# Second attention: feature forms of q and k by transposes of the token forms instead of a second projection

## The chip, the cores and the metric

One Trainium2 chip; the kernel runs on one of its cores. A core has a matrix engine (TensorE, "PE" in the profile), a vector engine (VectorE, "DVE"), an activation engine (ScalarE, "ACT"), a general engine (GpSimd, "POOL"), and a sync engine (SyncE, "SP") that issues most transfers. Each works through its own queue in order. The metric is the device time of one execution in microseconds. Before the change the median of three runs was 689.84 us (688.49 to 690.34).

## The reference, cut to what matters

Two layers. Each takes a layer norm of x, an attention s of it and a gated expert network g, and returns x + s * silu(g). x is 4 batches of 512 tokens with 128 features. The change lies in the attention of the second layer, which has 16 heads of 8 features and 16 channels:

```python
def proj(W, b):
    y = jnp.einsum('bse,ef->bsf', x, W) + b
    return y.reshape(B, S, H, D).transpose(0, 2, 1, 3)
Q = proj(Wq, bq)
K = proj(Wk, bk)
V = proj(Wv, bv)
cos_pm = jnp.cos(phase_modulators)

def wl_step(acc, wl):
    cpm, iw = wl
    m = cpm[None, :, None, None]
    scores = jnp.einsum('bhqd,bhkd->bhqk', Q * m, K * m) * SCALE
    scores = scores * jnp.cos(KERR * scores * scores)
    out = jnp.einsum('bhqk,bhkd->bhqd', jax.nn.softmax(scores, axis=-1), V)
    return (acc + out * iw, None)
```

The channels differ in a factor on the scores alone. The kernel computes a few functions of the scores (two exponentials, and powers up to the cube) once, and mixes them for each channel.

## The kernel before

The program is one stream of instructions for each engine, in an order that the code writes down: the helpers `mm1`, `act1`, `vec1`, `pool1` and `dma1` pin what they issue to the order of the program, so an instruction that waits holds up everything behind it on its engine. Most of them record one line each for all their calls (L356 for matmuls, L359 for activations, L379 for SP's transfers), so the profile is read by tile names.

It has three stages: the first layer up to about 303 us, the experts of the second layer (`ffn1`, 303 to 409 us), and the second attention (`attn1`, from 409 us).

**What a batch of the second attention needs.** `prepare1(b, ...)` gives the preparation of batch b as a table of steps, numbered by when they run. A step is a matmul part, an optional eviction and a rest.

- `tokens(w)`: the token form, tokens on the partitions. Four matmuls into the PSUM tile `ptq`, `ptk` or `ptv`; DVE adds the bias (L1407). Of k it makes the tile `tokk`, which holds every feature twice for the cubes; of q the tile `tokq`, which POOL squares (L1419); of v the values in `strip`.
- `project(w)`: the feature form, features on the partitions. One matmul of 512 columns from the same normed input into `pjq` or `pjk`; ACT adds the bias `b1` and evicts it to `qT` or `kT`. POOL then splits it into three bf16 parts (L1486, L1488: `part0` to `part2`, with the rest of the split in `left`), and SP writes the parts to DRAM (`kd`, `qd`). Of q, SP also writes tables of the feature form (`qe`, `qf`, in `table`).
- `cubes`, `forms`, `turned`: the products of the features of k (DVE, tile `feat`), sums of them over the tokens (PE, `pl`), and their transposes (PE, `pf`; DVE, `lin`).
- `sizes(w)`: bounds of the sums of squares (DVE).

The part tiles have one buffer each, so the first part of q waits until that of k has been written to DRAM. `spare` hands out the tiles `tokq` and `left` from two buffers.

**When the steps run.** Batch 0 is prepared in `ffn1`, one step for each expert pair from position 5 of `between` on (`prep`, `prepare`), as PE, ACT and DVE go through the experts; the first step of batch 1, `tokens("k")`, comes last. In `attn1`, iteration i of 64 does 16 iterations for each batch: four matmuls for scores (`s`), 32 for the sums over the keys (`acc`), the exponentials and squares (`e`) on ACT, some of the squares on DVE. In it, iteration t of batch b runs step t of batch b+1 and step t-16 of batch b+2, and `mixing`, which turns the sums of a finished head group into outputs:

- t = 8 `bank1` (`b`), 10 `sums1` (`den`; DVE takes the reciprocal `inv`), 11 `output1` of the batch before (`po`, `y`), 13 and 14 `quotients1` (`mix`; DVE multiplies to `pr`).

All the matmul parts of steps and mixing share the tag "mix" with two buffers. The matmul part of iteration i is issued in it, its rest in iteration i+1. The loads from DRAM (`first`, `second`, `third`, and `k`, `q`) stand in SP's queue at fixed iterations, between the writes of the preparation.

The table of steps (L1592):

```python
steps = {
    -7: [tokens("k")], -4: [], 0: [tokens("v"), project("k"), cubes(0)], 1: [project("q")],
    2: [forms(0), cubes(1)], 3: [tokens("q")], 4: [forms(1), cubes(2)],
    5: [sizes("k")], 6: [sizes("q")], 7: [turned(0), forms(2), cubes(3)],
    9: [forms(3)], 10: [turned(1)],
}
```

For b > 1, step -4 also holds the second half of the products of k (`quads`, L1429).

Of the kernel before, what the change touches and what calls it, by code (L numbers as in the profile page):

```python
# [12 lines left out]
F32 = mybir.dt.float32  # L13
# [4 lines left out]
ALU = mybir.AluOpType  # L18
# [3 lines left out]
P = 128  # L22
# [80 lines left out]
def bc(ap, axis, n):  # L103

    shape = list(ap.shape)
    return ap.unsqueeze(axis).to_broadcast(shape[:axis] + [n] + shape[axis:])


class Kernel:
# [124 lines left out]
    def load_second(self, pool, aside):  # L234

        nc, i = self.nc, self.i
        self.w1, self.b1, self.wt, self.bt = {}, {}, {}, {}
        for w in ("q", "k", "v"):
            own = aside.tile([P, D], F32, name=f"l1w{w}")
            nc.sync.dma_start(out=own, in_=i[f"L1_attn_W{w}"])  # L240

            flat = aside.tile([P, D], F32, name=f"l1b{w}f")
            nc.gpsimd.dma_start(out=flat, in_=i[f"L1_attn_b{w}"].partition_broadcast(P))
            self.wt[w] = pool.tile([P, D], F32, name=f"l1w{w}t")
            self.bt[w] = pool.tile([P, D], F32, name=f"l1b{w}t")
            for to, src in ((self.wt[w], own), (self.bt[w], flat)):
                nc.gpsimd.tensor_copy(
                    to.rearrange("p (m r d) -> p m r d", m=4, r=4),
                    src.rearrange("p (r m d) -> p m r d", m=4, r=4),
                )  # L250
            if w != "v":
                self.b1[w] = pool.tile([P, 1], F32, name=f"l1b{w}")
                own = i[f"L1_attn_b{w}"].rearrange("(r m d o) -> m r d o", m=4, r=4, o=1)
                for m in range(4):
                    nc.gpsimd.dma_start(out=self.b1[w][m * 32 : m * 32 + 32], in_=own[m])
        self.b1["o"] = pool.tile([P, D], F32, name="l1bo")
        nc.gpsimd.dma_start(out=self.b1["o"], in_=i["L1_attn_bo"].partition_broadcast(P))
        self.load_phases(aside)

        self.pm_hw = pool.tile([P, 2], F32, name="pm_hw")  # L260
        self.iw_hw = pool.tile([P, 1], F32, name="iw_hw")
        phases = i["L1_attn_phase_modulators"].rearrange("w (q m o) -> o q w m", o=2, q=4)

        self.wo_rep = pool.tile([P, 4, D], F32, name="wo_rep")
        nc.gpsimd.memset(self.wo_rep, 0.0)
        wo = i["L1_attn_Wo"].rearrange("(q u d) f -> q d u f", u=4, q=4)
        for q in range(4):
            for o in range(2):
                rows = slice(o * 64 + q * WL, o * 64 + (q + 1) * WL)
                nc.gpsimd.dma_start(out=self.pm_hw[rows], in_=phases[o, q])  # L270
                nc.gpsimd.dma_start(
                    out=self.iw_hw[rows], in_=i["L1_attn_interference_weights"].unsqueeze(1)
                )
            for j in range(3):
                at = q * 32 + j * 9
                nc.sync.dma_start(out=self.wo_rep[at : at + D1], in_=wo[q])
# [1097 lines left out]
    def prepare1(self, b, xnT, psum, tag):  # L1374
# [11 lines left out]
        def spare(what):  # L1386
            return pool.tile([P, S], F32, name=f"{what}{b}", tag="left", bufs=2)
# [8 lines left out]
        def tokens(w):  # L1396
            def pe():
                ps = psum.tile([P, 4, D], F32, name=f"pt{w}{b}", tag=tag[0], bufs=tag[1])
                for k in range(4):
                    self.mm1(  # L1400
                        ps[:, k, :], lhsT=toks[:, k, :], rhs=self.wt[w],
                        start=True, stop=True,
                    )
                return ps

            def biased(dst, ps):
                self.vec1(nc.vector.tensor_tensor(  # L1407
                    dst, ps.rearrange("p k (h d) -> p k h d", d=D1),
                    bc(self.bt[w].rearrange("p (h d) -> p h d", d=D1), 1, 4), ALU.add,
                ))  # L1410

            def rest(ps):
                if w == "v":
                    biased(own[:, :, :, 0:D1], ps)
                    return
                if w == "q":
                    t = spare("tokq").rearrange("p (n d) -> p n d", d=D1)
                    biased(t.rearrange("p (h k) d -> p k h d", k=4), ps)
                    self.pool1(nc.gpsimd.tensor_mul(t, t, t))  # L1419
                    now["squares" + w] = t  # L1420
                    return
                twice = pool.tile([P, 4 * H1, 2 * D1], F32, name=f"tok{w}{b}", tag="tok")
                t = twice[:, :, 0:D1]
                biased(t.rearrange("p (h k) d -> p k h d", k=4), ps)
                eng, pin = (nc.gpsimd, self.pool1) if b < 2 else (nc.vector, self.vec1)
                pin(eng.tensor_copy(twice[:, :, D1 : 2 * D1], t))

                def quads(at):
                    pin(eng.tensor_tensor(  # L1429
                        feat[:, :, at : at + 4], bc(t, 2, 4), moved(twice, SECOND[at], 2, 4),  # L1430
                        ALU.mult,
                    ))
                now["squares" + w], now["twice_k"] = feat[:, :, 0], twice
                now["quads"] = quads
                quads(0)
                if b < 2:
                    quads(4)
            return pe, rest
# [4 lines left out]
        def sizes(w):  # L1443
            def rest(_):
                size = pool.tile([P, H1, 4], F32, name=f"size{w}{b}", tag="size")
                self.vec1(nc.vector.tensor_reduce(
                    size.rearrange("p h k -> p (h k)"), now["squares" + w], AX.X, ALU.add
                ))
                self.vec1(nc.vector.tensor_reduce(
                    norms[:, int(w == "k"), b], size, AX.X, ALU.max  # L1450
                ))
            return (lambda: None), rest

        def project(w):
            def pe():
                ps = psum.tile([P, S], F32, name=f"pj{w}{b}", tag=tag[0], bufs=tag[1])
                self.mm1(ps, lhsT=self.wt[w], rhs=toks, start=True, stop=True)
                return ps

            def evict(ps):  # L1460
                t = pool.tile([P, S], F32, name=f"{w}T{b}", tag=f"{w}T")
                self.act1(t, ps, AF.Identity, bias=self.b1[w])
                return t

            def rest(t):
                if w == "q":


                    now["once"] = self.a1d.tile(
                        [4, D1, 4, S], F32, name=f"qe{b}", tag="qe"  # L1470
                    )
                    now["table"] = self.a1d.tile(
                        [4, TABLE, 2, 4, S], F32, name=f"qf{b}", tag="qf"
                    )
                    now["rows"] = t
                    if b == 0:
                        for m in range(4):
                            table(m)[1](None)

                dram = now["parts" + w] = self.a1d.tile(  # L1480
                    [P, 2, 4, S], BF16, name=f"{w}d{b}", tag=f"{w}d"
                )
                left = spare("left" + w)
                for k in range(3):
                    part = pool.tile([P, S], BF16, name=f"part{w}{b}_{k}", tag=f"part{k}")
                    self.pool1(nc.gpsimd.tensor_copy(part, t))  # L1486
                    if k < 2:
                        self.pool1(nc.gpsimd.tensor_sub(left, t, part))  # L1488
                        t = left
                    for x, at, end, step in STAND[w][k]:  # L1490
                        n = len(range(at, end, step))
                        self.dma1(dram[:, x, at:end:step], bc(part, 1, n))
            return pe, rest, evict

        def table(m):
# [70 lines left out]
        def turned(mm):  # L1566
# [23 lines left out]


        steps = {  # L1592
            -7: [tokens("k")], -4: [], 0: [tokens("v"), project("k"), cubes(0)], 1: [project("q")],
            2: [forms(0), cubes(1)], 3: [tokens("q")], 4: [forms(1), cubes(2)],
            5: [sizes("k")], 6: [sizes("q")], 7: [turned(0), forms(2), cubes(3)],
            9: [forms(3)], 10: [turned(1)],
        }
# [806 lines left out]
    def run(self):  # L2404
# [15 lines left out]
        with tc.tile_pool(name="wf1", bufs=1) as wf1, tc.tile_pool(name="f1", bufs=1) as f1:  # L2420
# [13 lines left out]
            with tc.tile_pool(name="ap", bufs=1, space=PSUM) as psum:  # L2434
# [13 lines left out]
                def begin():  # L2448
# [10 lines left out]
                    for at, each in steps.items():  # L2459
                        prep.extend(each if at == 0 else [each] if each else [])  # L2460
                    ahead = self.prepare1(1, first.xnT, psum, ("w", 4))
                    prep.extend([ahead[-7]])

                def prepare():
                    each = prep.pop(0)
# [26 lines left out]
                    18: [(f.up2, B - 1, NE // 2 - 1), (self.opening1, psum, "w", 4)],  # L2492
                    19.5: [(self.opened1, psum, "w", 4)],
                }
                for k in range(14):
                    between.setdefault(5 + k, []).append((prepare,))
                for k in range(4):
                    between.setdefault(13 + k, []).append((f.fetch, 1, 2 * k, 2))
# [75 lines left out]
```

## Time and profile before

| what | value |
| --- | --- |
| median of three runs | 689.84 us |
| the profiled execution | 691.6 us, of it span 689.9 us |
| chain that ended last | PE 74%, DVE 14%, ACT 8%, DMA 2% of the span |
| pjq and pjk (8 matmuls) | 16 records, 592 ns median |
| ptq, ptk, ptv | 32 records each, 275 ns median |
| kT, qT (ACT) | 4 each, 0.70 and 0.69 us |
| tokk, tokq (DVE, biased) | 4 each, 0.69 us |
| squares of q (POOL) | 4, 1.04 to 1.21 us |

A matmul of f32 leaves two records in the profile, a transpose of f32 one. Records of PE overlap, so what a group takes is read from its start to the start of the next one, not from the durations. "Idle before" in a line is the time that the engine waited ahead of the instruction, with what ended it. The span is that of the core's instructions; the execution's time has 1.7 us around it.

### The profile page before, as it was taken

The numbers are of one execution on the slowest core, as the hardware profiler recorded it, in microseconds if no ns is written. First come the engines' busy times: TensorE is split into PE (matmuls) and PEld (weight loads), VectorE is DVE, ScalarE is ACT, GpSimd is POOL, SyncE is SP. The second block draws the span as 40 slices with busy tenths as digits, with TensorE's granted clock in tenths as the row PEclk, the third lists the DMA queues.
The fourth block names the chain that finished last, engine by engine and source line by source line (L and its number), as shares of the span: only waits on it lengthen the run. The fifth ranks groups of instructions, "written<-read, shape, count | busy, mean of one in ns | idle before, by whom it ended". The sixth has DMA issues, their size and how long they took to land.

```text
span 689.9 us, 23790 instructions
## 1 busy us (share of the span) xinstructions
PE 656.5 (95%) x10123; PEld 411.0 (60%) x10123; DVE 501.9 (73%) x1084; ACT 487.2 (71%) x806; POOL 349.1 (51%) x383
## 2 busy tenths in 40 slices
PE   8999999999999898899999999999999999999995
PEld 4666667988978768777778863333335243422424
DVE  6866476686677958865378225979898999678884
ACT  4433478797787787643554369988997999899850
POOL 7590046767767575873753243312584753321170
PEclk9999999999999999999999999999999999999998
DMA  6850153233233131100034359777849694956300
GB/s 169 155 149 0 68 150 96 49 110 95 51 105 99 35 95 34 34 2 1 4 122 159 96 164 251 204 192 162 236 153 212 154 243 133 223 137 164 77 17 20
DMA packets 85489, 79.72 MB, mean 116 GB/s; under 512 B 42640, under 2 KB 74160, under 8 KB 82304
## 3 DMA queue, kind: packets, MB, share of 16 engines
q1 hardware_dynamic: 82544, 75.39, 41.5%
q0 software_dynamic: 2256, 2.47, 1.9%
q8 instruction: 82, 1.34, 0.8%
q10 hardware_dynamic: 576, 0.26, 0.2%
q14 instruction: 31, 0.25, 0.1%
HBM read 51.62 MB, written 26.21 MB: 113 GB/s over the span
## 4 chain that ended last, share of the span: by engine, by line
PE 74%; DVE 14%; ACT 8%; DMA 2%; issue 1%; POOL 0%; SPq 0%; DVEq 0%; ACTq 0%; POOLq 0%
PE acc L356 9%; PE eo L356 8%; PE pp L356 7%; ACT e L359 7%; PE po L356 6%; PE ph L356 5%; PE pv L356 4%; PE b L356 3%; PE s L356 3%; PE pl L356 3%; PE dot L356 2%; PE pg L356 2%; PE pu L356 2%; PE sc L356 2%; DVE elu L709 2%; PE mu L356 2%
## 5 line engine op out<-in xcount | busy, mean ns | idle before, releaser
L359 ACT ACTIVATE e<-s 128x1024 f32<-128x1024 f32 x124 | 122.2, 1059 | 14.5 <-PE s L356 14.1
L356 PE MATMUL acc<-e,strip 128*32 128x512 f32 x1000 | 123.7, 598 | 0.9 <-DVE e L1969 0.9
L359 ACT ACTIVATE e<-e 128x1024 f32<-128x1024 f32 x104 | 107.4, 1095 | 0.0
L763 POOL TENSOR_TENSOR t<-t,gate 128x512 f32<-128x512 f32 x32 | 52.3, 1634 | 52.8 <-DVE t L744 52.8
L356 PEld LDWEIGHTS acc<-e,strip 128*32 128x32 f32 x1000 | 28.2, 109 | 70.0 <-issue 59.0
L801 POOL TENSOR_TENSOR t<-t,gate 128x512 f32<-128x512 f32 x32 | 50.1, 1566 | 25.9 <-DVE sums L800 22.2
L359 ACT ACTIVATE pj<-pp 128x512 f32<-128x512 f32 x64 | 38.5, 602 | 19.3 <-PE pp L356 17.7
L709 DVE SCALAR_TENSOR_TENSOR elu<-elu,up 128x512 f32<-128x512 f32 x60 | 47.5, 791 | 0.2
L359 ACT ACTIVATE h<-ph 128x1024 f32<-128x1024 f32 x20 | 20.5, 1025 | 35.9 <-PE ph L356 32.1
L356 PE MATMUL s<-q,k 64*128 64x512 bf16 x256 | 41.1, 382 | 3.6 <-ACT e L359 3.3
L356 PEld LDWEIGHTS <-k 64*128 64x128 bf16 x256 | 8.7, 94 | 59.9 <-issue 58.1
L802 POOL TENSOR_TENSOR t<-t,t 128x512 f32<-128x512 f32 x32 | 42.2, 1320 | 2.5
L686 DVE TENSOR_TENSOR E<-sc,cap 128x512 f32<-128x512 f32 x32 | 22.0, 688 | 29.0 <-PE sc L356 29.0
L356 PE MATMUL eo<-w_out,h 128*128 128x128 f32 x320 | 39.7, 278 | 0.0
L356 PEld LDWEIGHTS eo<-w_out,h 128*128 128x128 f32 x320 | 37.7, 192 | 3.4 <-issue 2.4
L359 ACT ACTIVATE elu<-pj 128x512 f32<-128x512 f32 x60 | 38.5, 642 | 0.1
L359 ACT ACTIVATE up<-pj 128x512 f32<-128x512 f32 x60 | 38.4, 640 | 0.0
L1750 POOL TENSOR_TENSOR pr<-pr,pr 128x512 f32<-128x512 f32 x14 | 22.5, 1632 | 30.5 <-DVE pr L1745 30.4
L359 ACT ACTIVATE attT<-tn 128x128 f32<-128x128 f32 x100 | 19.6, 282 | 20.9 <-PE tn L722 19.9
L356 PE MATMUL pp<-xnT,l0Wk 128*64 128x128 f32 x512 | 31.4, 280 | 3.0 <-issue 2.2
L1657 DVE TENSOR_TENSOR second<-second,first 128x1024 f32<-128x1024 f32 x16 | 26.7, 1672 | 9.6 <-DMA second<-qf 9.6
L356 PE MATMUL po<-l0wo,attT 64*128 64x128 f32 x512 | 31.9, 281 | 0.3 <-DVE t L744 0.3
(353 smaller groups left out, 1589.4 us busy)
## 6 DMA issues: line engine op xcount, KB each, us to landing
vd<-vt SPq DMA_DIRECT2D x32, 256.0 KB
vone<-vd SPq DMA_DIRECT2D x64, 128.0 KB
first<-qe SPq DMA_DIRECT2D x8, 1024.0 KB
second<-qf SPq DMA_DIRECT2D x16, 512.0 KB
third<-qf SPq DMA_DIRECT2D x32, 256.0 KB
qf<-qT SPq DMA_DIRECT2D x64, 64.0 KB
k<-kd SPq DMA_DIRECT2D x16, 256.0 KB
q<-qd SPq DMA_DIRECT2D x16, 256.0 KB
```

Source lines behind the costliest of these rows:

```text
L356: return self.pin(self.nc.tensor.matmul(*args, **kw))
L359: return self.pin(self.nc.scalar.activation(*args, **kw))
L686: self.vec1(nc.vector.tensor_tensor(e, ps[:, :, 0:256].rearrange("p x (hp c) -> p x hp c", hp=4), bc(bc(self.cap, 1, 4), 1, 2), ALU.min,))
L709: self.vec1(nc.vector.scalar_tensor_tensor(t, t, 1.0, up, ALU.min, ALU.add))
L763: nc.gpsimd.tensor_mul(t, t, self.gate)
L801: nc.gpsimd.tensor_mul(t, t, gate2)
L802: nc.gpsimd.tensor_add(t, t, seg[n]["t1"])
L1657: self.vec1(self.nc.vector.tensor_mul(t, t, self.first1[mm][:, two]))
L1750: self.nc.gpsimd.tensor_add(self.prod1[b, m], self.prod1[b, m], t)
```

## The change

The bias of the feature form and its loads go: `b1` of q and k, eight small DMAs issued by POOL. `tokens` now keeps a token form with the features of each head group side by side, (k h d), as `tokens` + w: for q in place of the former order, for k by a second biased add from the same PSUM tile. `project` makes the feature form from it by four 128x128 transposes, and ACT evicts with Copy and no bias. The first squares of q on POOL move behind the split of q, since the transposes read the token form; `sizes("q")` reads them in the new order. The split of k subtracts in place. `tokens("q")` moves from step 3 to step -4: for batch 0 from behind `forms(0)` to behind `tokens("k")`, for batch 1 to the end of `ffn1`, for batches 2 and 3 to iteration 12 of the batch two before. In `ffn1`, `tokens("v")`, both `project`, `cubes(0)` and `forms(0)` of batch 0 each come one position later.

```diff
-            if w != "v":
-                self.b1[w] = pool.tile([P, 1], F32, name=f"l1b{w}")
-                own = i[f"L1_attn_b{w}"].rearrange("(r m d o) -> m r d o", m=4, r=4, o=1)
-                for m in range(4):
-                    nc.gpsimd.dma_start(out=self.b1[w][m * 32 : m * 32 + 32], in_=own[m])
...
                 if w == "q":
-                    t = spare("tokq").rearrange("p (n d) -> p n d", d=D1)
-                    biased(t.rearrange("p (h k) d -> p k h d", k=4), ps)
-                    self.pool1(nc.gpsimd.tensor_mul(t, t, t))
-                    now["squares" + w] = t
+                    t = now["tokens" + w] = spare("tokq").rearrange(
+                        "p (k h d) -> p k h d", k=4, d=D1
+                    )
+                    biased(t, ps)
                     return
...
                 biased(t.rearrange("p (h k) d -> p k h d", k=4), ps)
+                now["tokens" + w] = spare("tokk").rearrange("p (k h d) -> p k h d", k=4, d=D1)
+                biased(now["tokens" + w], ps)
...
-                self.vec1(nc.vector.tensor_reduce(
-                    size.rearrange("p h k -> p (h k)"), now["squares" + w], AX.X, ALU.add
-                ))
+                sums = size.rearrange("p h k -> p k h" if w == "q" else "p h k -> p (h k)")
+                self.vec1(nc.vector.tensor_reduce(sums, now["squares" + w], AX.X, ALU.add))
...
-                ps = psum.tile([P, S], F32, name=f"pj{w}{b}", tag=tag[0], bufs=tag[1])
-                self.mm1(ps, lhsT=self.wt[w], rhs=toks, start=True, stop=True)
-                return ps
+                ps = psum.tile([P, 4, P], F32, name=f"pj{w}{b}", tag=tag[0], bufs=tag[1])
+                for k in range(4):
+                    self.pin(nc.tensor.transpose(
+                        ps[:, k], now["tokens" + w][:, k].rearrange("p h d -> p (h d)"), self.ident
+                    ))
+                return ps.rearrange("p k s -> p (k s)")
...
-                self.act1(t, ps, AF.Identity, bias=self.b1[w])
+                self.act1(t, ps, AF.Copy)
...
-                left = spare("left" + w)
+                left = spare("left" + w) if w == "q" else t
...
+                if w == "q":
+                    t = now["squares" + w] = now["tokens" + w]
+                    self.pool1(nc.gpsimd.tensor_mul(t, t, t))
...
-            -7: [tokens("k")], -4: [], 0: [tokens("v"), project("k"), cubes(0)], 1: [project("q")],
-            2: [forms(0), cubes(1)], 3: [tokens("q")], 4: [forms(1), cubes(2)],
+            -7: [tokens("k")], -4: [tokens("q")], 0: [tokens("v"), project("k"), cubes(0)], 1: [project("q")],
+            2: [forms(0), cubes(1)], 3: [], 4: [forms(1), cubes(2)],
...
-                    prep.extend([ahead[-7]])
+                    prep.extend([ahead[-7], ahead[-4]])
...
-                for k in range(14):
+                for k in range(15):
                     between.setdefault(5 + k, []).append((prepare,))
```

## The prediction

> **What bounds the kernel now.** I read the page's busy shares first, then the chain of waits in order of time, then the busy time of each engine in stretches cut where the chain changes engine, and last the timelines of PE, DVE, ACT, POOL and SP around each instruction that the change moves.
>
> ```profile
> PE 656.5 (95%) x10123; PEld 411.0 (60%) x10123; DVE 501.9 (73%) x1084; ACT 487.2 (71%) x806; POOL 349.1 (51%) x383
> ...
> PEclk9999999999999999999999999999999999999998
> ```
>
> PE looks like the bound everywhere, at a granted clock that never falls. The stretches say otherwise; columns are length, then busy us of PE, PEld, DVE, ACT, POOL (instructions), granted clock, DMA share, GB/s:
>
> ```profile
> 411.00:440.00 29.00, 26.74 (x296) 9.94 (x292) 18.46 (x28) 28.05 (x35) 13.24 (x12) 1.00 1.01 240
> 463.00:471.00 8.00, 7.16 (x47) 2.07 (x46) 8.00 (x8) 8.00 (x10) 0.00 (x0) 1.00 1.05 210
> 486.00:515.00 29.00, 28.95 (x410) 12.20 (x410) 26.72 (x39) 28.29 (x36) 18.93 (x17) 1.00 0.67 195
> 546.00:577.00 31.00, 30.60 (x330) 11.20 (x324) 30.30 (x41) 30.50 (x38) 17.09 (x16) 1.00 0.79 205
> ```
>
> In 486-515 and 546-577, where the projections of batches 2 and 3 stand, ACT has 0.71 and 0.50 us left, hardly more than PE. PE there ends last, but little is gained by a shorter PE alone. From 411 to 463 ACT and the DMAs bind (DMA share 1.01), and at 463 the chain hangs on DVE:
>
> ```profile
> 462.96 1.28 DVE third L1668
> 464.24 1.67 DVE inv L1718
> 465.91 0.57 DVE bank L2017
> 466.48 2.20 DVE feat L1429
> 468.67 1.20 DVE third L1668
> 469.87 0.61 DVE pr L1745
> 470.48 0.04 issue
> 470.52 1.72 PE mix L356 x4
> ```
>
> From 303 to 409 the chain is PE nearly without a break: there a microsecond of PE is a microsecond.
>
> **The price of each operation.**
>
> ```profile
> 334.03 1.04 PE L986 MATMUL lnt<-ident,xn 128*128 128x128 f32 x8
> 334.90 1.06 PE L356 MATMUL ptv<-l1wvt,xnT 128*128 128x128 f32 x8
> ...
> 341.24 1.13 PE L356 MATMUL pjk<-xnT,l1wkt 128*128 128x512 f32 x2
> 342.20 1.95 PE L356 MATMUL eo<-w_out,h 128*128 128x128 f32 x16
> ```
>
> Each reading is from one start to the next. Eight transposes take 0.87 us, so the four that replace a projection take 0.435. A projection takes 0.96 here and 0.86, 0.95, 1.06, 0.95, 1.06, 0.96, 1.05 at its seven other places: 7.85 in all against 8 x 0.435 = 3.48. PE loses 4.37 us of work. For the transposes of the token forms, which this trace doesn't hold, I take the lnt row, the same shape and operation; the other bound is its 273 ns each in line, 1.09 a group, which would be a small loss.
>
> The Trainium skill (TensorE: Matmul & The Clock Gate, Part 4: PE-mode transpose) gives about 275 ns for a 128x128 transpose inside a kernel, and says that transposes don't count as busy for the clock gate. Taken as a serial cost, an estimate from that page, a group would cost 1.10 us, and my sum below would end near +1.3 instead of 0. The rows have 273 ns as duration but 109 ns as pitch, at a granted clock of 1.00, so they decide.
>
> DVE adds one biased add per batch, the second order of k: 128x512 from PSUM, 0.69 us by the row of the first (0.60 to the next start), 2.8 us in all. ACT: kT and qT last 0.70 and 0.69 with a bias tile; the Copies of this shape (bank, eg) 0.60: 8 x 0.1 less. The squares on POOL and the subtraction, now in place, keep their shapes and rows (1.05 and 1.17), and sizeq, now read with a stride, is bounded by sizek, which reads with a stride already: 0.67 against 0.68. POOL loses eight DMA issues at 8.5-14.7 us, 2.37 + 2.31 = 4.7 us; POOL then idles 16.6 us before to_mix at 68.7, so it isn't on the path.
>
> **The change by stage.**
>
> *A, up to 409.* pjk and pjq of batch 0 save 0.52 + 0.42 = 0.94 where PE binds. Each comes a step later, and their waits (pjk on the second biased add, three steps back; pjq on tokq, four steps back) are long over. qe/qf/qd leave SP some 3 us later, at 357-373 instead of 354-370, with rows<-eg behind them; k and q are loaded at 393.7, so some 20 us cover it, and the indirect loads of POOL keep 8 of their 10 us before joined. forms(0) moves to ptq's old place, and cubes(1) still fits ahead of pl_1 (DVE ends it at 367.0, PE wants it at 367.1); without that cover it would cost its 2.5 us. Against this, tokens("q") of batch 1 enters between the last eo groups: ptk at 401.3 takes 0.99 there, and the eo behind it, DVE's eg and the DMA that ACT's e waits for all come later. Net +0.05.
>
> *B, 411-463.* ptq(1) leaves PE at 424.8 and kT/qT save ACT 0.2, but the stretch ends on the DMA of third, issued by SP behind qf: 0. DVE's new add at 453.9 is eaten by its 2.9 us wait for that DMA.
>
> *C, 463-471.* tokens("q") of batch 2 now runs at iteration 12 and its add at 13, on DVE between bank and feat of the chain above: +0.60 for pr and so for mix. PE's own 1.09 at 463.1 fits beside that (it idles 0.45 and 0.29 there, and the rest is less than 0.60).
>
> *D, 471-515.* PE saves 0.51 + 0.62 + 1.09 (ptq(2) is gone from iteration 3). What the stage can take is ACT's gap ahead of qT, 0.55, and the two shorter evictions, 0.20: -0.75.
>
> *E, 515-546.* DVE's second add at 520.9 is covered by its 1.44 us wait for po; were that cover gone, 0.6. At iteration 12 ptq(3) enters PE at 533.8 for 1.09, and DVE, done with bank at 532.8, waits for it until 534.9; feat, third and pr stand behind that add, and PE's mix waits for pr. DVE: add to 535.5, feat 2.2 and third 1.2 at their rows without a busy POOL (whose y ends earlier while DVE waits), pr 0.6 each: 539.5 and 540.1. PE: 1.09 less the 0.3 us by which it is ahead of ACT: mix at 540.4 instead of 539.6. PE decides: +0.80. With DVE at its rows beside POOL (2.9 and 2.3), pr comes at 541.2: up to +1.8.
>
> *F, 546-577.* As D: PE saves 2.2, ACT's gap is 0.50 and the evictions 0.20: -0.70. After it nothing is changed.
>
> Sum: 0.05 + 0 + 0.60 - 0.75 + 0.80 - 0.70 = 0.0 us. It is made on the profiled execution, 691.6 us (span 689.9, 1.7 around it); that lies 1.8 above the median of the runs, 689.84, so I forecast **689.8 us** as the median.
>
> **Rivals.** *The PE saving comes through.* If ACT can run ahead in D and F, PE's work decides: 0.05 + 0.60 - 2.2 + 0.80 - 2.2 = -3.0, 686.8 us. For it: PE is the chain's engine in both. Against: ACT is busy without a gap from 487.1 to 514.8 and from 555.4 to 583.4.
>
> *The new wait on DVE decides (slower).* Place: iteration 13 of batches 0 and 1. DVE stands 2.05 us for ptq(3), then 0.60 for the add, and feat, third and pr run beside POOL as before; with batch 0, where PE's whole 1.09 shows: 0.05 + 1.09 + 2.65 = +3.8, 693.6 us, provided that D and F give nothing back because DVE (30.3 of 31.0 us busy in F) holds them. It decides once pr of iteration 13 ends later than 540.4.
>
> *Transposes cost as much as the projection* (the upper bound of 1.09, 273 ns each in line): A becomes 0.99 + 0.13 + 0.23 = +1.35, and the sum +1.3; 691.1. The change then doesn't do what it says, but the time hardly tells.
>
> **How the numbers follow.** A measurement of this kernel can tell about 0.3%, 2.07 us, from no change. My forecast and the third rival lie within that: together 0.43 (0.38 and 0.05). The first rival, and anything else that lets PE's 4.4 us through, 0.25; the DVE wait and other late starts behind the moved steps 0.32, more than the gain because each moved step adds a wait, and coupled stages pass on delays more readily than savings. The range reaches to both rivals: 686.8 to 693.6. The likeliest case's own range: upwards with PE's whole 1.09 in C and 1.8 in E, +1.5; downwards with ACT's next gaps behind D and F, 0.49 at 515.3 and 0.85 at 584.2, closed as well, -1.3: 688.5 to 691.3.
>
> **What would show it.** In the changed profile: pjk and pjq as four matmuls with ident at a pitch near 0.11 us; ACT without its gap ahead of qT; add tokq between bank and feat near 466 and 535, with a DVE wait for ptq of some 2 us at the second; mix at the second not before 540; ACT's e at 412 unmoved. I am wrong if ACT's stretch 471-515 shrinks by over 1.5 us, if mix of iteration 14 is more than 1.5 us late in either batch, or if e at 412 moves by over 0.5 us.

## The result and the profile after

The changed kernel takes 699.74 us (698.79 to 700.56) against 689.22 for the kernel before on the same chip: ratio 1.0150, 95% interval 1.0134 to 1.0167. A later measurement gave 1.0129 (1.0114 to 1.0143). The forecast was no change; the change costs some 1.4%, about 10 us, far outside the range. The profiled execution has a span of 697.9 us, 8.0 more than that of before; the profiled execution of before (691.6) lay 2.4 above the median 689.22, this one (699.57) at its median, hence the difference.

The first part of the page after the change shows almost nothing of this: every engine's busy time is within 5 us of what it was, and PE has less work. The second line below is PE's busy tenths in 40 slices of the span.

```profile
PE 655.0 (94%) x10139; PEld 410.0 (59%) x10139; DVE 506.7 (73%) x1088; ACT 486.0 (70%) x806; POOL 346.2 (50%) x375
PE   7999999999999888799979998999999999999995
```

One digit of PE fell by two, the 7 of slice 21 (349 to 366 us, in the experts). The chain of waits, in order of time, runs there through ACT and DVE, where it ran on PE without a break before (columns: start, us, what):

```profile
344.00 1.74 PE ph L351 x8
...
346.87 1.25 ACT L354
...
351.79 1.13 DVE feat L1521
352.91 1.10 DVE feat L1525
354.01 0.20 DVE feat L1529
354.21 2.80 DVE feat L1533 x3
357.01 0.11 DVE place L1065
...
360.72 2.58 DVE one L1085 x2
363.31 0.05 issue
363.35 1.46 PE px L351 x3
```

DVE runs the router of batch 2 (the choice of two experts for each token, up to `top` and `gates`), then `feat`, the products of k of `cubes(0)`, then the places of the tokens (`place`, `own`) and the marks `one`. PE gathers rows by them (`px`). The order on DVE is the same in both kernels. What differs is how long the instructions take. First the kernel before, then the changed one, on DVE's timeline (start, us, engine, line, operation, tiles, shapes, count; in brackets the idle time ahead of it):

```profile
351.38 1.22 DVE L1519 TENSOR_TENSOR feat<-tokk,feat 128x1024 f32<-128x1024 f32 x1
352.51 0.22 DVE L1523 COPY feat<-tokk 128x128 f32<-128x128 f32 x1
...
352.85 1.09 DVE L1531 TENSOR_TENSOR feat<-tokk,feat 128x256 f32<-128x256 f32 x3
354.18 0.19 DVE L1070 SCALAR_TENSOR_TENSOR place<-pn,mask 128x32 f32<-128x32 f32 x1 [0.24 <-PE pn L356]
...
357.01 4.27 DVE L1090 TENSOR_TENSOR one<-places,place 128x512 bf16<-128x512 f32 x4
```

```profile
351.70 1.21 DVE L1521 TENSOR_TENSOR feat<-tokk,feat 128x1024 f32<-128x1024 f32 x1
352.83 1.18 DVE L1525 COPY feat<-tokk 128x128 f32<-128x128 f32 x1
...
354.14 2.87 DVE L1533 TENSOR_TENSOR feat<-tokk,feat 128x256 f32<-128x256 f32 x3
356.93 0.18 DVE L1065 SCALAR_TENSOR_TENSOR place<-pn,mask 128x32 f32<-128x32 f32 x1
...
360.63 5.12 DVE L1085 TENSOR_TENSOR one<-places,place 128x512 bf16<-128x512 f32 x4
```

The copy takes 1.18 us in place of 0.22 and the three products 2.87 in place of 1.09; `place` comes 2.75 us later and `one` ends 4.5 us later. The reason stands on POOL, which was idle from 347.7 to 354.5 before the change (the first line is the kernel before, the others the changed one):

```profile
354.50 0.61 POOL L1486 CAST partq<-qT 128x512 bf16<-128x512 f32 x1 [6.85 <-ACT qT L359]
```

```profile
349.06 0.61 POOL L1485 CAST partk<-kT 128x512 bf16<-128x512 f32 x1 [5.95 <-ACT kT L354]
...
351.74 2.19 POOL L1487 TENSOR_TENSOR kT<-kT,partk 128x512 f32<-128x512 f32 x1
353.99 0.69 POOL L1485 CAST partk<-kT 128x512 bf16<-128x512 f32 x1
```

With project k of batch 0 one position later, its eviction kT stands behind ACT's reload of tables for the router (1.25 us in the chain above) and ends at 349.0, not at 343.1, so POOL's split of k falls on the router. The two engines take turns: DVE's first product (351.70 to 352.91) keeps its 1.21 us while POOL's subtraction, begun with it, takes 2.19 in place of 1.16; then DVE's copy, at 352.83, ends only as that subtraction does.

PE's `px` waits for `one`, and after the wait the granted clock is halved (PE's timeline before, which has no wait, and after; then the stretches of the changed kernel: length, busy us and instructions of PE, PEld, DVE, ACT, POOL, then the clock, DMA share, GB/s):

```profile
359.23 1.46 PE L356 MATMUL px<-one,xp 128*128 128x512 bf16 x6
```

```profile
361.79 1.17 PE L351 MATMUL px<-one,xp 128*128 128x512 bf16 x3 [4.25 <-DVE one L1085]
363.35 1.46 PE L351 MATMUL px<-one,xp 128*128 128x512 bf16 x3 [0.40 <-DVE one L1085]
```

```profile
362.00:363.00 1.00, 0.96 (x3) 0.10 (x1) 1.00 (x1) 0.01 (x1) 0.94 (x2) 0.55 0.25 76
363.00:364.00 1.00, 0.65 (x2) 0.28 (x3) 1.00 (x2) 0.59 (x1) 1.00 (x2) 0.50 0.26 96
364.00:365.00 1.00, 1.00 (x3) 0.66 (x2) 1.00 (x2) 0.15 (x1) 1.00 (x1) 0.50 0.25 82
365.00:366.00 1.00, 1.00 (x3) 0.30 (x2) 0.97 (x3) 0.45 (x1) 0.21 (x1) 0.74 0.26 100
```

The six px take 2.42 us and the ph behind them 2.17, against 1.29 and 1.72 before: 1.58 more for the halved clock, beside 4.65 of waiting.

To see where the rest lies, marks of each profile are set against the kernel before, each counted from the first ph of its experts (303.71 before). The kernels other than "changed" are those of the experiments below; each row is one profiled execution. The marks are starts of ACT's `second`, ends of the last `eg`, starts of the first `e` behind it, of DVE's second, eighth, tenth and thirteenth `inv`, and the end of the span. The table shows how much later each comes, in us:

| kernel | second | last eg | e | inv 2 | inv 8 | inv 10 | inv 13 | end |
| --- | --- | --- | --- | --- | --- | --- | --- | --- |
| time before, from that ph | 103.30 | 105.60 | 108.24 | 160.45 | 255.59 | 292.76 | 345.10 | 386.19 |
| changed | 5.82 | 6.40 | 8.01 | 4.94 | 6.94 | 8.26 | 7.22 | 8.19 |
| changed, second profile | 6.77 | 7.35 | 9.08 | 8.68 | 10.67 | 11.97 | 10.24 | 10.39 |
| filler | 5.82 | 5.82 | 5.82 | 4.55 | 5.21 | 5.21 | 5.20 | 5.09 |
| quiet_pool | 0.79 | 1.37 | 3.40 | 0.33 | 3.34 | 4.08 | 2.26 | 4.65 |
| k_first | 0.38 | 0.96 | 2.74 | 0.89 | 2.15 | 3.48 | 1.85 | 2.10 |
| k_first_q1 | 0.06 | 0.06 | 0.08 | -0.24 | 1.85 | 2.86 | 1.19 | 0.93 |
| tables_first | 5.52 | 6.10 | 8.27 | 5.21 | 8.28 | 5.63 | 7.09 | 7.29 |
| best3 | 0.06 | 0.06 | 0.07 | -0.65 | 0.39 | -2.28 | -0.82 | -0.44 |

Most of the loss of the changed kernel is there at `second`, before the second attention has begun. `e` is later still by 1.6, which has been recovered by inv 2. The second attention, 110 to 345 us behind that ph, then adds less than 1 us to what stood at the last eg. The second profile, of the later measurement (after_again), agrees up to e within some 1 us, but recovers only 0.4 by inv 2 and is 2.9 later at inv 13 than at its last eg; it was the slowest of its five executions (702.08 against a median of 698.11). So what the table says of the experts is firm to about 1 us, what it says behind e to some 3.

The last two of the stretches that the prediction read, 486-515 and 546-577, are taken 6.82 us later here. They look as they did before, with ACT at 28.55 us and now without any gap in the second:

```profile
492.82:521.82 29.00, 28.32 (x412) 11.34 (x408) 26.02 (x39) 28.55 (x38) 18.09 (x17) 1.00 0.67 195
552.82:583.82 31.00, 30.05 (x396) 12.89 (x392) 29.49 (x40) 31.00 (x39) 19.02 (x17) 1.00 0.75 200
```

### The profile page after: what moved, and what is told of

Read it like the earlier page. It is cut to its first block, busy times and chain, and to the rows that moved or that the text cites. A ratio compares the mean times of both kernels' runs of the same rounds, so it can differ in the third digit from the quotient of the medians.

```text
span 697.9 us, 23826 instructions
## 1 busy us (share of the span) xinstructions
PE 655.0 (94%) x10139; PEld 410.0 (59%) x10139; DVE 506.7 (73%) x1088; ACT 486.0 (70%) x806; POOL 346.2 (50%) x375
## 4 chain that ended last, share of the span: by engine, by line
PE 63%; DVE 15%; ACT 12%; DMA 4%; issue 3%; SPq 2%; POOL 1%; DVEq 0%; POOLq 0%; ACTq 0%
ACT e L354 10%; PE eo L351 7%; PE pp L351 7%; PE acc L351 6%; PE po L351 5%; PE ph L351 5%; PE pv L351 4%; PE b L351 3%; PE s L351 2%; DMA kd<-partk 2%; PE sc L351 2%; DVE elu L704 2%; SPq L374 2%; PE pg L351 2%; PE pu L351 2%
## 5 line engine op out<-in xcount | busy, mean ns | idle before, releaser
L351 PE MATMUL acc<-e,strip 128*32 128x512 f32 x1000 | 125.9, 598 | 1.2 <-DVE e L1971 0.9
```

Of the source, the lines that this page charges most:

```text
L351: return self.pin(self.nc.tensor.matmul(*args, **kw))
```

## The experiments

Ratios are to the kernel before on the same chip, with 95% intervals; four chips were used.

### Is it POOL beside DVE?

**quiet_pool.** The rest of project k of batch 0 (split and writes) and the split of the normed input of batch 3 move behind the split of q:

```diff
+                late, done = [], []
...
                     each = prep.pop(0)
+                    done.append(each)
                     for pe, rest, *evict in each if isinstance(each, list) else [each]:
                         ps = pe()
+                        if len(done) == 4:
+                            late.append((rest, evict[0](ps)))
+                            continue
                         after = rest(evict[0](ps) if evict else ps)
+                        if len(done) == 6:
+                            first.split(3)
+                            late[0][0](late[0][1])
...
-                    9.5: [(f.placed, 2), (f.split, 3)] + marks(2, 0, 1),
+                    9.5: [(f.placed, 2)] + marks(2, 0, 1),
```

> The changed kernel with one thing moved, on POOL (and SP's writes with it): the split of k of batch 0 and the split of the normed input of batch 3 stand behind the split of q, so POOL is idle while DVE runs the router of batch 2 (from top at 349 us) and cubes(0). PE's, ACT's and DVE's orders stay those of the changed kernel. Theory (POOL at work beside DVE made the same DVE instructions longer, so place, own and one end 4.5 us late and PE's px stands 4.65 us idle and then runs at half clock): feat of cubes(0) is back at about 2.6 us in place of 5.3, place starts near 354.3 in place of 356.93, PE's wait ahead of px falls from 4.65 to 1 us or less, the granted clock in 362-366 does not fall to 0.5, and the time falls by 4.5 to 6 us, to about 694.5. Rival (PE's order: the sums of forms(0) and ptq, 2.4 us, stand no longer ahead of px, and POOL is innocent): px still waits over 4 us, time 699.7 within 0.7.

Measured: 695.85 us, ratio 1.0089 (1.0063 to 1.0115), that is 0.0061 or 4.2 us less than the changed kernel. On DVE and PE:

```profile
352.11 0.22 DVE L1525 COPY feat<-tokk 128x128 f32<-128x128 f32 x1
...
353.45 0.18 DVE L1065 SCALAR_TENSOR_TENSOR place<-pn,mask 128x32 f32<-128x32 f32 x1
...
354.94 2.90 DVE L1085 TENSOR_TENSOR one<-places,place 128x512 bf16<-128x512 f32 x4
```

```profile
357.12 1.46 PE L351 MATMUL px<-one,xp 128*128 128x512 bf16 x5
```

With POOL idle (until 356.68, beside the last of the four `one`) the copy is back at 0.22 us, `one` takes 2.90 us (less than the 4.27 of before the change, where POOL split q beside it), and px waits for nothing, with PE's order left as the change made it. The theory's price for the time was 4.5 to 6 us; 4.2 differs from it by less than the intervals. The rival, PE's order, is out.

**filler.** The kernel before, with POOL kept busy where it idled:

```diff
+                if w == "k" and b == 0:
+                    for k in range(5):
+                        self.pool1(nc.gpsimd.tensor_mul(left, left, left))
```

> The kernel before with five further products of 128x512 on POOL (1.16 us each, 5.8 us, results unused) behind the last part of k of batch 0, in the 6.85 us in which POOL idles there (347.7-354.5). Nothing on PE, ACT or DVE is changed. Theory (POOL beside DVE): feat of cubes(0) grows from 2.6 to about 5 us, place and one come 2 to 4 us later, px gets a wait of 2 to 3 us in place of none, time +2 to +5 us, to 691 to 694. Rival (PE's order): DVE and px stay where they are, time 689.2 within 0.7.

Measured: 693.33 us, ratio 1.0049 (1.0028 to 1.0070), +3.4 us. DVE's three products of `feat` take 2.46 us and `one` starts at 359.84, although this execution was 1.5 us ahead. PE then waits at three places:

```profile
356.26 1.09 PE L356 MATMUL pl<-feat,strip 128*32 128x129 f32 x32 [1.24 <-DVE feat L1534]
357.29 2.05 PE L356 MATMUL eo<-w_out,h 128*128 128x128 f32 x16
360.99 0.81 PE L356 MATMUL px<-one,xp 128*128 128x512 bf16 x2 [1.65 <-DVE one L1090]
362.56 1.46 PE L356 MATMUL px<-one,xp 128*128 128x512 bf16 x3 [0.76 <-DVE one L1090]
```

Five idle-time products on POOL, which nobody reads, cost the kernel before a third of what the change costs in time; in the one profile, from the first ph on, they cost 5.1 us at the end. That is the mechanism by itself, with none of the change.

**k_first.** The changed kernel, with the place of project k in the experts as it was:

```diff
+                        if at == 0:
+                            each = [each[1], each[0], each[2]]
                         prep.extend(each if at == 0 else [each] if each else [])
...
-                    9.5: [(f.placed, 2), (f.split, 3)] + marks(2, 0, 1),
+                    9.5: [(f.placed, 2)] + marks(2, 0, 1),
...
-                    10.5: sends(2, 0, 1), 11: sends(2, 2, 3),
+                    10.5: [(f.split, 3)] + sends(2, 0, 1), 11: sends(2, 2, 3),
```

> The changed kernel with project k of batch 0 ahead of tokens v (so at the position it had before the change; kT near 342 us in place of 348.4, the split of k on POOL at 343-348) and the split of the normed input of batch 3 behind the split of q, as POOL had them before the change. Theory (POOL beside DVE): POOL is idle from 348 to qT at some 356, DVE's chain is as before the change, px waits 1 us or less, time 5 to 7 us less than the changed kernel, 693 to 694.7. Rival (PE's order): forms(0) and ptq are still not ahead of px, so px still waits over 4 us, 699.7 within 0.7.

Measured: 693.12 us, ratio 1.0047 (1.0031 to 1.0063), 7.1 us less than the changed kernel. DVE's `one` takes 2.90 us again and px doesn't wait. One swap of two steps and one of a split on POOL take back two thirds of the loss.

What is left shows the same effect once more. POOL's splits, moved out of the way of `cubes(0)`, now run beside `cubes(1)`. DVE's copy and three products there took 0.22 and 1.09 us in the kernel before (at 365.85 and 366.19), and the sums over them, `pl`, waited for nothing. In k_first:

```profile
363.92 1.18 DVE L1525 COPY feat<-tokk 128x128 f32<-128x128 f32 x1
365.23 2.46 DVE L1533 TENSOR_TENSOR feat<-tokk,feat 128x256 f32<-128x256 f32 x3
```

```profile
367.75 1.09 PE L351 MATMUL pl<-feat,strip 128*32 128x129 f32 x32 [0.72 <-DVE feat L1533]
```

Counted from the first ph, PE is 0.88 us ahead of the kernel before at the ph ahead of that sum (364.53 against 366.21) and 0.06 behind at the eo after it (368.78 against 369.52): the PE time that the transposes saved in the experts is gone. The wait, 0.72 or 0.73 us, is in all seven profiles of versions of the changed kernel with POOL idle beside `cubes(0)`. None of these has POOL idle beside both.

### The late e, the tables, and what is left

**k_first_q1.** k_first, with tokens q of batch 1 behind the last eo:

```diff
-                for k in range(15):
+                for k in range(14):
                     between.setdefault(5 + k, []).append((prepare,))
...
                 self.ffn1(first, between, True)
+                prepare()
```

> The kernel k_first with tokens q of batch 1 behind the last eo of the experts, in place of between the last eo groups. In k_first ACT's e still starts at 413.89, 1.94 us later than before the change, although its PE reached the same s 0.4 us earlier: 0.9 is ptq between the eo groups, and the last eg waits 4.4 us for e in place of 2.64. Theory (ptq inside the chain costs its 0.9 us and moves the write of the last rows into a worse place beside the load of first): e starts 0.9 to 2.5 us earlier, at 411.4 to 413, and the ratio to the kernel before falls from 1.0047 to about 1.002. Rival (the longer wait behind the last eg has nothing to do with ptq): e gains 0.9 at most, ratio 1.0034 or above.

Measured: 692.66 us, ratio 1.0047 (1.0031 to 1.0064). The wait went as the theory had it, the time didn't. First the changed kernel, then this one; between the last eg and e stand a write of its rows and e's wait for it:

```profile
414.83 0.69 DVE L1126 COPY eg<-eo 128x512 f32<-128x512 f32 x1 [1.77 <-PE eo L351]
416.09 0.59 SPq L374 DMA_DIRECT2D first<-qe  x1
419.77 1.06 ACT L354 ACTIVATE e<-second 128x1024 f32<-128x1024 f32 x1 [5.20 <-DMA rows<-eg]
```

```profile
411.45 0.69 DVE L1126 COPY eg<-eo 128x512 f32<-128x512 f32 x1 [1.77 <-PE eo L351]
...
414.80 1.06 ACT L354 ACTIVATE e<-second 128x1024 f32<-128x1024 f32 x1 [3.02 <-DMA rows<-eg]
```

From the end of eg to e it is 4.25 us in the first and 2.66 in the second. In all seven profiles with tokens q of batch 1 between the eo groups it is 4.25 to 4.90, in the nine others 2.64 to 2.66. One reading, which no run tests, is that the loads of the second attention start with eg, not with e, and bind at inv 2, where k_first had already recovered 1.9 of e's 2.74. The profile is 1.2 us better at its end, and a gain of that size in time would fit the intervals too.

**tables_first.** The changed kernel, with all writes of the tables of q ahead of the writes of its parts:

```diff
-                    if b == 0:
-                        for m in range(4):
-                            table(m)[1](None)
+                    for m in range(4):
+                        table(m)[1](None)
...
-        if b:
-            for m in range(4):
-                steps[2 + m].append(table(m))
```

> The changed kernel with the writes of the tables of q (qe, qf) of batches 1 to 3 ahead of the writes of its parts in SP's queue (all four tables at once, as batch 0 has them), so SP need not stand for POOL's split of q: for batch 3 SP idled 567-575 and then issued 24 transfers back to back until 599. In the second attention the changed kernel was up to 2.9 us ahead of the kernel before (relative to e at 412) until 588 and lost this again at 594-604, where PE's s and DVE's third wait for transfers. Theory (SP's chain of issues, which began 0.8 us late behind POOL's split of q, sets that point): third lands several us earlier and 1.5 to 3 us of the lead are kept, 697 to 698.2. Rival (the transfers themselves fill the DMA engines there, so the order of issue is of no account): 699.7 within 0.7; a loss of 1 us or more if the earlier table writes delay loads of batch 0 or 2 that are waited for.

Measured: 698.52 us, ratio 1.0114 (1.0088 to 1.0140), which overlaps with both intervals of the changed kernel, so the time is no evidence. In the profile the theory's first half holds: DVE's `third`, which waited 2.41 us for its load, doesn't wait, and inv 10 comes at 5.63 in place of 8.26. Its second half falls: at inv 13 it is 7.09 in place of 7.22. What SP gave, the next stage took.

**before_tables.** The same edit on the kernel before.

> The kernel before with only the order of SP's writes changed as in tables_first. In it SP idles 563.2-566.4 for POOL's split of q of batch 3 and then issues without a break until 593, and DVE's third at 594.9 waits 0.42 us for its load (2.41 in the changed kernel). Theory (SP's chain sets the point at 594-604 only for a kernel that is ahead of it): no change, 689.9 within 1 us. Rival (SP's chain sets the end of both kernels): 1 us or more faster than the kernel before.

Measured: 689.38 us, ratio 1.0000 (0.9988 to 1.0011): no change, as the theory had it.

**best3.** k_first, k_first_q1 and tables_first together, timed on two chips.

> k_first, tokens q of batch 1 behind the last eo, and the tables of q of batches 1 to 3 written ahead of its parts, together. Theory (the three causes stand one behind the other in time, and their gains add): ratio to the kernel before 0.997 to 1.001. Rival (the end is set by the transfers of the second attention, which begin at the same time anyway): as k_first_q1 alone, 1.002 to 1.0034.

> best3 once more, as the partner on the same chip of best3_loads_again: ratio 1.003 to 1.006, first pp 69 us or more behind the first lnt.

Measured: 692.01 us, ratio 1.0044 (1.0029 to 1.0059), and 690.70 us, 1.0017 (1.0005 to 1.0029). From the first ph to the end it takes 0.44 us less than the kernel before in the one profile and 0.58 less in the other; in time it is still 1 to 3 us behind. The first ratio is above both theories, the second between them (and under the 1.003 to 1.006 expected of the repeat). That a part of the loss lies ahead of the experts was a guess from this. A profile is one execution: that of before was 2.4 us over its median, the first of best3 the fastest of its six (689.83 against 692.01), so the gap between profiles and times may be nothing more. A candidate stood in the first 35 us: without the eight loads of biases POOL issues its next small loads, `pm_hw` and `iw_hw`, at 15 to 29 us in place of 29 to 37, beside the first weights.

**late_bias, after_loads, best3_loads.** The kernel before with the eight loads moved behind `pm_hw` and `iw_hw`; the changed kernel and best3 with the eight loads kept, unused.

```diff
+            if w != "v":
+                self.b1[w] = pool.tile([P, 1], F32, name=f"l1b{w}")
...
+                for m in range(4):
+                    nc.gpsimd.dma_start(out=self.b1[w][m * 32 : m * 32 + 32], in_=own[m])
```

> The kernel before with the eight small loads of the biases of q and k (POOL, 8.5-14.7 us) moved behind the loads pm_hw and iw_hw, so that POOL issues everything behind them as early as it does in the changed kernel (pm_hw and iw_hw from some 15 us in place of 29); nothing else differs. In the profiles the first eo of the experts to the lnt of the third batch (14.6 to 31.3 before, 15.4 to 33.0 after) and the first pp (75.5, 75.2, 74.8 in three profiles with the loads, 77.3, 76.6, 76.4, 76.2, 79.5, 76.4 in six without) stand later without the loads. Theory (POOL's small loads, issued earlier, meet the loads of the first weights; wd lands later): +1 to +2.5 us against the kernel before, ratio 1.0015 to 1.0036, first pp at 76.2 or later. Rival (POOL idles until 68.7, so what it issues early is of no account, as the prediction had it): ratio within 0.001 of 1.

> The changed kernel with the eight small loads of the biases of q and k kept where they were (their tiles are not read), so that POOL's early issues stand as before the change. Theory (early loads): 1 to 2.5 us less than the changed kernel, ratio 1.0115 to 1.0135 in place of 1.015, first pp near 75.2. Rival: ratio 1.014 to 1.016.

> best3 with these eight loads kept as well: project k of batch 0 early and POOL idle beside the router, tokens q of batch 1 behind the last eo, tables of q ahead of its parts. From the first ph of the experts to the end the profile of best3 took 0.44 us less than that of the kernel before, so what best3 loses (ratio 1.0044) should lie ahead of 303 us. Theory (early loads): ratio 0.998 to 1.001. Rival (the loss lies elsewhere): 1.003 or above.

Measured on a third chip, on which the kernel before took 694.85 us: ratios 1.0022 (1.0005 to 1.0038), 1.0136 (1.0116 to 1.0157) and 1.0103 (1.0084 to 1.0122). The last is far worse than best3; its profile shows PE standing between matmuls at a place where no engine is waited for:

```profile
384.74 0.39 PE L356 MATMUL pl<-feat,strip 128*32 128x129 f32 x2 [1.09 <-issue]
385.48 0.27 PE L356 MATMUL pl<-feat,strip 128*32 128x129 f32 x1 [0.35 <-issue]
...
387.60 0.43 PE L356 MATMUL pl<-feat,strip 128*32 128x129 f32 x3 [1.00 <-issue]
```

So the pairs were timed once more, each with its partner, on a fourth chip:

> best3_loads once more, on another chip: in its first profile PE stood and crept at 383.6-394 in the sums of forms and the eo behind them, with no other engine as the cause (8 us, 4.2 us at the same place in late_bias on that chip, none in the seven profiles of the two chips before), so its ratio there says nothing of the loads. Theory (the early loads of the biases keep POOL's later small loads out of the way of the first weights, worth 1 to 2.5 us): 1 to 2.5 us less than best3_again, ratio 0.998 to 1.002, first pp some 68.3 us behind the first lnt. Rival (the loads are of no account): within 0.7 us of best3_again.

> The changed kernel once more, as the partner on the same chip of after_loads_again: ratio 1.0134 to 1.0167, first pp 69 us or more behind the first lnt.

> The changed kernel with the eight loads kept, once more. Theory (early loads): 1 to 2.5 us less than after_again, ratio 1.011 to 1.0135. Rival: within 0.7 us of after_again.

Measured: best3_loads 1.0032 (1.0018 to 1.0046) against best3 1.0017 (1.0005 to 1.0029); the changed kernel with the loads 1.0145 (1.0130 to 1.0160) against 1.0129 (1.0114 to 1.0143) without (a little under the 1.0134 expected of it). Both are slower with the loads, if anything. The theory of the early loads falls. The 1.0022 of late_bias stays without an explanation; its profile has such a stall too, and whether the kernel before has it on that chip no profile shows.

## Why the prediction was wrong

**A, up to 409 (+0.05 forecast, +6.4 at the last eg, +8.0 at e).** This is the step that failed. "Each comes a step later, and their waits ... are long over" asked whether the moved steps' inputs are ready. It didn't ask what their outputs start, nor what then runs beside what: the overlap was wrong. Project k ends in a split on POOL, six us later than before, on the router's DVE chain; "the squares on POOL and the subtraction ... keep their shapes and rows" priced POOL's work at rows from other company, and DVE's work in this stretch was not priced at all, since the change doesn't touch it. Yet the prediction knew the effect: stage E takes DVE's feat and third once "without a busy POOL" (2.2 and 1.2) and once "beside POOL" (2.9 and 2.3). The kernel before had it in the very copy of this stretch, at another place (duration in ns: shortest, median, longest of 16):

```profile
L1523 DVE COPY feat<-tokk x16: 208/220/1178, 352.5 to 581.0; 128x128 f32<-128x128 f32 x16
```

The ledger of PE, from start to start, up to the second `s` ahead of the attention (405.99 before, 412.20 after; 6.40 later from the first ph): the work of pjk and pjq with what moved beside them -0.88 (forecast -0.94), tokens q of batch 1 +0.89 (forecast +0.99), px's waits for `one` +4.81 (4.41 and 0.40; the trace counts 4.25 of the first as idle), the halved clock +1.58. (`second`, which ACT starts on this `s`, is 5.82 later, since it was not waiting for PE before.) The terms that were priced are right to 0.1 us; the two that weren't are the result.

A "cover" was named for `cubes(1)`; the one that failed stands behind `cubes(0)`. Its last instructions are `place` and the four `one`, and px needs the first of these for its first three matmuls and the second for the next three (in the changed kernel they start some 0.05 us after these end). Before, the second `one` ended at 359.25 and the fourth px started at 359.87: 0.6 us were to spare. After the change `one` came 4.2 us later, and PE, with forms(0) now behind px, was ready for it 1.7 us earlier. The cover of `cubes(1)` itself, 0.1 us by the prediction (367.0 against 367.1), held in the changed kernel, where PE was late, and fails by 0.72 or 0.73 us in every version that takes the first wait away; there the forecast saving is lost too.

**e at 411.95 "unmoved".** It moved by 7.8, which the prediction named as the sign of its error. 1.6 of these are the longer write of the last rows when ptq stands between the eo groups; they were recovered by inv 2 in this profile.

**B, 411 to 463 (0).** Right in kind: the stretch ends on a transfer, and it swallowed e's 1.6 us and more (8.01 to 4.94); in the second profile 0.4 (9.08 to 8.68).

**C to F, 463 to 577 (-0.05).** From the last eg to inv 13 the changed kernel loses 0.8 (6.40 to 7.22; 2.9 in the second profile) and k_first 0.9, and best3 gains 0.9. Most details are as forecast: pjk and pjq at a pitch of 0.12 (347.54 to the eo at 348.03), qT on ACT without a gap ahead of it, the add of tokq between bank and feat at 471.57 and 540.47, and there a DVE wait of

```profile
540.47 0.69 DVE L1402 TENSOR_TENSOR tokq<-ptq,l1bqt 128x512 f32<-128x512 f32 x1 [2.06 <-PE ptq L351]
```

2.06 us where 2 were forecast. "After it nothing is changed" was wrong by 1.3 us at inv 10, where `third` came late behind POOL's split of q and SP's 24 issues; tables_first takes 2.6 us off there, and it is of no use at inv 13.

**The rivals.** "Transposes cost as much as the projection" is out (0.43 to 0.59 us a group). "The PE saving comes through" is out: the projections themselves are shorter at every place, but the time does not follow. In the experts the waits above take the saving, and from the last eg to inv 13 no profile gains more than 1 us. The rival on the slower side named a DVE wait, in iteration 13; it exists, at the length that was said, and isn't the cause. The chance of slower was 0.32, for that wait "and other late starts behind the moved steps"; POOL beside DVE was not among its reasons. One reading of the clock was wrong: "a granted clock that never falls" rests on slices of 17 us. In the first layer of the kernel before it was halved twice for some 3.4 us, once here:

```profile
259.00:263.00 4.00, 3.49 (x58) 3.37 (x60) 3.83 (x10) 0.69 (x2) 1.90 (x2) 0.57 0.24 56
```

Nothing in the sum rests on it; a price for a halved clock behind a wait was missing.

**What the rows and the pages said.** On the transposes the rows decided rightly (0.43 to 0.59 us a group, not the 1.10 estimated from the 275 ns of TensorE: Matmul & The Clock Gate, Part 4, as a serial cost). The rule that bore on this change stands on another page of the Trainium skill, SBUF — State Buffer, section "SBUF: two separate sides": VectorE and GpSimd share a pair of ports under an exclusive lock, and whoever starts first holds it for its whole instruction; VectorE takes part with instructions in a mode that uses two ports, or with two inputs in SBUF while GpSimd reads SBUF. This case's rows agree (a copy of 0.22 us held until a 2.19 us subtraction of POOL ended). Read beside the change's moved step it would have been the question to ask.

**What stays open.** best3, with the first wait and the late e mended, is level with the kernel before from the experts on in each profile, and 0.17 to 0.44% slower in time. So the cause is shown for the two thirds that k_first takes back; some 3 of the 10 us remain there without a shown cause. The timed executions have no stage times, and the early loads, which the first 80 us of the profiles seemed to point to, were not it. No version here beats the kernel before; one with POOL idle beside `cubes(1)` as well was not run.

## What to carry to other kernels

When a step moves, follow it to its last instruction: ask, for each engine that its tail lands on, which other engine's critical chain runs beside it now. VectorE and GpSimd work is not priced by its own rows alone; look for the stretch in which one of them was idle and the other on the path, and take that idle time for a resource that the kernel uses. A cover is to be looked for on every chain of the stage that the moved work touches, and the tightest is the one where the two sides of a wait arrive closest together.

## What the runs showed of the hardware

- DVE beside a busy POOL: one of the four products of `one` took 0.68 us with POOL idle, and 1.09, 1.10, 1.52 or 1.64 beside POOL's casts, subtractions and squares. All four took 2.90 in quiet_pool (POOL idle beside the first three), 3.87 in filler (idle beside the last two), 4.27 in the kernel before and 5.12 in the changed one (at work nearly throughout in both, with other instructions). A copy of 128x128 took 0.22 or 1.18.
- The halved clock needs no long single idle stretch. In the changed kernel 0.50 was granted after one wait of 4.25 us. In filler it was granted from some 362.5 on, after waits of 1.24, 1.65 and 0.76 us within 9 us; of the 3.4 us ahead of 362.5 PE was idle for 2.3, in two pieces (columns as in the stretches above). The Trainium skill (TensorE: Matmul & The Clock Gate, Part 1) speaks of an idle window of some 3.4 us; the first agrees with that, the second shows that the window need not be idle throughout.

```profile
362.00:364.00 2.00, 1.44 (x4) 0.81 (x5) 1.97 (x5) 0.44 (x1) 0.00 (x0) 0.62 0.26 94
364.00:366.00 2.00, 2.00 (x4) 0.83 (x3) 1.73 (x16) 0.60 (x1) 0.00 (x0) 0.53 0.26 100
```

- On one of the chips PE stood up to 1.09 us at a time between matmuls of one group, with no engine as the cause, at the same place in two of three kernels; the profiles of the other chips have nothing like it there. The ratio of best3_loads taken on it, 1.0103, was 1.0032 elsewhere.
